# A decoder layer on one core: a softmax reciprocal moved behind the values' sums, the first pair's products in four banks, and one experts' product moved into slot 14

## The chip, the cores and the metric

The kernel runs on one core of a Trainium2 chip. The metric is the device time of one execution in microseconds. The kernel before was timed three times: 862.58, 862.88 and 864.7 us, median 862.88. A further execution was recorded by the hardware profiler. Its own time is 862.72 us, of which 860.9 us lie between its first and its last instruction (the span), so 1.8 us lie around the span.

The engines are PE (matrix products and transposes through the identity), DVE, ACT and POOL (elementwise work) and SP (which here only issues transfers). PEld is the part of PE that loads the stationary operand of a product.

## The reference

One decoder layer for 16 sequences of 128 tokens with 256 features, all in float32. Cut to what matters:

```python
x = x + self_attention(layernorm(x))        # 16 heads of 64, with biases, no mask
x = x + cross_attention(layernorm(x), ctx)  # 16 heads of 16, keys masked by position
x = x + experts(layernorm(x))

def experts(x):                             # 8 experts, 256 -> 512 -> 256
    logits = x @ gate_w.T + gate_b          # then RMS-normalized over the 8 experts
    g = max(softmax(logits / 0.5))          # the largest gate of each token
    norm_g = g / (g + 1e-6)
    h = gelu(einsum('nd,edh->neh', x, w1) + b1)
    y = einsum('neh,ehd->ned', h, w2) + b2  # every expert is computed for every token
    return (y * norm_g[:, None, None]).sum(axis=1)
```

## The kernel before

**Slots.** The first half of the span is attention. It is written as 16 slots, one for each sequence (a tile of 128 tokens). Slot s holds the self-attention of sequence s, the cross-attention queries and scores of sequence s-1, the cross-attention values of sequence s-2, and the projections for a coming pair of sequences. In the profile the first scores (L694) of slots 1, 2, 3, 13, 14 and 15 start at 49.06, 73.44, 100.81, 374.77, 401.91 and 427.19 us; a slot takes about 27.4 us. The second half of the span is the experts.

**The order is written out by hand.** Every step of a slot is an event with a name, and a table gives each name its due time: `DUE` for an ordinary slot, `FIRST_DUE` for slot 0, `SECOND_DUE` for three changes in slot 1. A slot has the length `SLOT`. `run_slots` takes all events in the order of their due times and lets each issue its instructions; on each engine the instructions then stand in exactly this order, and each engine works through its own in order. A smaller number in the table thus puts a step further ahead on its engine; the number itself is no time on the chip. A step that is due after the end of its slot lies between the steps of the next one: `xn=34.27` is 7.29 in the next slot.

**Pairs by seven products.** Queries, keys and values of two sequences are computed together with seven products of half-size blocks instead of eight (a Strassen scheme). For the values this is `paired_values`: four steps `v1x`, `v1y`, `v2x`, `v2y` on PE, one half of the heads per slot, and sums on ACT and DVE between them. For queries and keys it is `paired_steps`, with `q1x`, `q1y`, `q2x`, `q2y` and the same for k, and sums that carry the bias. The body for the values, cut:

```python
def first():                                   # v1x: bank with a and b
    product(1, v["a"]); product(6, v["b"])
    due("vu0", nc.scalar.copy, u[:, 0], v["a"])          # ACT
    plus("vu1", u[:, 0], u[:, 0], v["b"])                # DVE
def second():                                  # v1y: bank with f and e
    product(7, v["f"]); product(5, v["e"])
    plus("vu2", u[:, 1], u[:, 0], v["f"])
    plus("vu3", out[1][:, 1], u[:, 1], v["e"])
def third():                                   # v2x: product 2 onto a, then vc00 (ACT)
def fourth():                                  # v2y: product 4 onto f, product 3 onto e
```

Products 4 and 3 write onto the bank that `vu2` and `vu3` have read, so the first of them waits for `vu3`. In `paired_steps` the same place is `q2y` (or `k2y`), which waits for `qu3`, the sum written to `qT`. A float32 product is two PE rows in the trace, a transpose one.

**The softmax** (`softmax`, L395 to L416) has four steps for each half of eight heads: the negated maximum on DVE (`max0`), four exponentials with their sums on ACT (`ex0a`, `ex0b`), the reciprocal of the four sums on DVE (`r0a`, `r0b`, L412, `rinv`), and the normalization on POOL (`mul0a`, L416). The same names with c are cross-attention.

**Layer norms.** `bn` takes the statistics, `root` computes the inverse deviation with a chain of small DVE instructions (`inverse_root`, L323 to L338), and `xn` normalizes (L371). `LNx` transposes `xn` on PE (L380), and ACT copies the result (`LNxc`). `ab1` and `ab2` add a bias to `xs` on POOL, after the `xn` that reads it.

**PSUM.** Scores use four of the eight banks. All other products share four banks in the pool `ps_mm`; a tile gets a bank when the last reader of the tile in it is done. `ck` and `cke`, `cke2` are the cross-attention keys: the product and its four copies on ACT (L756, L767).

**Experts ahead of time.** The first 512 tokens' hidden values for 16 of 32 blocks are computed as plain products (`pre_hidden`, L1003, two products of 512 columns, four PE rows) while attention still runs. `PRE_STEPS` says which of them stand in which slot, by the event at whose due time they are issued and the event at which their bank is copied out: "qu1" means a copy on DVE, any other name one on ACT. The others stand in the tail, a stretch after slot 15 whose order is written out as calls.

Of the kernel before, what the change touches and what calls it, by code (L numbers as in the profile page):

```python
# [54 lines left out]
DUE = dict(  # L55
    S0=0.0, S1=1.0, T2a1=2.05, T2a2=2.49, T2a1e=2.69, ck=2.92, T2a2e=3.19, max0=3.47, v1x=3.79,
    cke=3.99, vu0=4.3, cke2=4.4, max1=4.61, v1y=4.66, q1x=5.52, ex0a=5.54, vu1=6.08, q1y=6.42,
    vu2=6.76, qu0=6.91, r0a=7.11, vu3=7.24, v2x=7.32, mul0a=7.39, vc00=7.4, ex0b=7.41, qu1=7.63,
    v2y=7.77, qu2=8.06, qu3=8.49, LNx=8.6, q2x=8.64, vc1=8.84, q2y=9.09, LNxc=9.1, ex1a=9.13,
    vc0=9.19, r0b=9.53, mul0b=9.81, qc1=10.19, cvr=10.21, qc00=10.51, qc0=10.54, r1a=10.98,  # L60
    T2b1=11.23, mul1a=11.26, cvre=11.31, ex1b=11.66, T2b2=11.66, T2b1e=11.86, CQ=12.1,
# [16 lines left out]
    r0a=-1.32, ex0b=-1.3, mul0a=-1.2, S1=-0.6, fv0e=0.1, r0b=0.15, mul0b=0.2, fab0=0.25,  # L78
# [3 lines left out]
    ve0=11.1, T1a2=11.34, T1a1e=11.54, T1b1=11.77, T1a2e=12.14, T1b2=12.21, LN1=12.64,  # L82
    T1b1e=12.74, LN1c=13.06, T1b2e=13.34, w0q=13.6, w0k=13.7, SVa=14.25, SVb=15.15, atT0=15.42,
    q1=17.2, atT1=17.21, wv0=17.3, q1e=17.6, k1=18.0, w1q=18.1, tf=18.2, SO=19.16, ke1=19.6,
    ws1=19.7, w1k=20.0, xsSO=22.81, bn=23.22, v1=23.47, ck=25.2, ve1=25.39, q1x=26.9, qu0=26.95,
    cke=27.0, cke2=27.01, q1y=27.8, qu1=28.2, k1x=28.7, qu2=28.8, qu3=29.2, root=29.25,
    xn=29.27, ab2=29.3, ku0=29.3, ab1=29.31, ku1=29.85, q2x=30.5, q2y=30.95, qc00=31.0,
    k1y=31.85, qc1=32.0, k2x=32.8, ku2=32.9, ku3=33.3, kc00=33.3, qc0=33.32, k2y=33.4, kc1=34.5,
    kc0=34.9,
)  # L90

SECOND_DUE = dict(wv1=4.7, st0=11.9, st1=12.46, st2=16.3, tf=19.6, st3=24.0)

PRE_STEPS = (
    (14, "q1x", "qc00"), (14, "k1x", "ku0"),
    (15, "v1x", "vu0"), (15, "q1x", "qu1"), (15, "k1x", "ku0"), (15, "k2x", "kc00"),
)
ON_ACT = ('T1a', 'T1b', 'T2a')
# [6 lines left out]
def decoder_layer(  # L105
# [53 lines left out]
    def psum_mm(name):  # L159
        return ps_mm.tile([P, 512], F32, tag="mm", name=name)  # L160
# [128 lines left out]
    def due(name, f, *a):  # L289

        if now[0] is None:
            with urgent():
                f(*a)
        else:
            at(name, f, *a)
# [449 lines left out]
    def cross_norm(b):  # L745
        xnT2 = work.tile([P, KD, 1, T], F32, tag="xnT2", name="xnT2")
        transpose_tokens([entry.pop(("xn", b))], xnT2, "LNxc")
        entry["xnT2", b] = xnT2
# [52 lines left out]
    def cross_queries(b):  # L801
        xnT2 = entry.pop(("xnT2", b))
        qT = work.tile([P, C2, T], F32, tag="q2T", name="q2T")
        mm = psum_mm("mm_q2")[:, : C2 * T].rearrange("p (m t) -> p m t", m=C2)
        for m in range(C2):
            for k in range(KD):
                nc.tensor.matmul(
                    mm[:, m, :],
                    wx[:, 0, k, m * P : (m + 1) * P],
                    xnT2[:, k, 0, :],  # L810
                    start=(k == 0),
                    stop=(k == KD - 1),
                )
        due(
            "q2T",
            nc.vector.tensor_tensor,
            qT, mm, bqk2[:, 0, :].unsqueeze(2).broadcast_to([P, C2, T]), ALU.add,
        )
        entry["q2T", b] = qT

    def cross_scores(b):


        qT, kT = entry.pop(("q2T", b)), entry.pop(("k2T", b))
        scs = [psum_sc(f"sc2_{n}") for n in range(2)]
        for m in range(C2):
            for r in range(4):
                rs = slice(32 * r, 32 * r + 32)
                nc.tensor.matmul(  # L829
                    scs[r // 2][:, r % 2, m * 2 * T : (m + 1) * 2 * T].rearrange(  # L830
                        "p (e t) -> p e t", e=2
                    ),
                    qT[rs, m, :],
                    kT[rs, m, :, :],
                    start=True,
                    stop=True,
                    tile_position=(32 * r, 0),
                )
        entry["sc2", b] = scs
# [13 lines left out]
    def cross_transposed(b, half, n):  # L853
        if n == 0:
            entry["cprT", b, half] = work.tile([P, 8, T], F32, tag="cprT", name="cprT")
        transposed(entry["cpr", b, half], entry["cprT", b, half], n, f"T2{'ab'[half]}{n + 1}e")

    def cross_values(b):


        v = v2s[b // GB % 2]
        prT = [entry.pop(("cprT", b, n)) for n in range(2)]
        po = psum_mm("po2")[:, : C2 * T].rearrange("p (m t) -> p m t", m=C2)
        for m in range(C2):
            for e in range(2):
                for r in range(4):
                    c0 = e * D + (4 * m + r) * 32
                    nc.tensor.matmul(  # L868
                        po[32 * r : 32 * r + 32, m, :],
                        v[:, b % GB, c0 : c0 + 32],  # L870
                        prT[r // 2][:, 4 * (r % 2) + 2 * m + e, :],
                        start=(e == 0),
                        stop=(e == 1),
                        tile_position=(0, 32 * r),
                    )
        atT = work.tile([P, C2, T], F32, tag="at2T", name="at2T")
        due(
            "at2T",
            nc.vector.tensor_tensor,
            atT, po, col(BV2, C2).unsqueeze(2).broadcast_to([P, C2, T]), ALU.add,  # L880
        )
        entry["at2T", b] = atT

    def cross_output(b):
        atT = entry.pop(("at2T", b))
        mm = psum_mm("mm_o2")
        for k in range(KD):
            nc.tensor.matmul(
                mm[:, :D], atT[:, k, :], wx_vo[:, 1, k, :], start=(k == 0), stop=(k == KD - 1)
            )  # L890
        due("xsCO", nc.vector.tensor_tensor, xs[:, b, :], mm[:, :D], xs[:, b, :], ALU.add)
# [29 lines left out]
    def expert_norm(b, copy=nc.scalar.copy):  # L921
        transpose_tokens(
            [entry.pop(("xn3", b))],
            xnT[:, :, b * T : (b + 1) * T].rearrange("p k (i t) -> p k i t", i=1),
            "LN3c",
            copy,
        )
# [67 lines left out]
    def pre_hidden(n, copy, name=None):  # L995

        p, i = n // 2, n % 2
        if n % 4 == 0:
            two = keep.tile([P, 2, 2, MT], F32, tag=f"k{(n // 4 + 3) % 4}", name="pre")
            pre[p], pre[p + 1] = two[:, 0], two[:, 1]  # L1000
        mm = psum_mm("mm_h")
        for k in range(KD):
            nc.tensor.matmul(  # L1003
                mm,
                w1q[p // (NP // QN)][:, i, k, p % (NP // QN)],
                xnT[:, k, :MT],
                start=(k == 0),
                stop=(k == KD - 1),
            )
        due(name, copy, pre[p][:, i], mm)  # L1010
# [150 lines left out]
    def sums():  # L1161
        return [ps_y.tile([P, 2, HT], F32, tag=f"y{n}", name=f"y{n}") for n in range(4)], set()
# [7 lines left out]
    def hidden_late(p):  # L1170
        for i in range(2):
            h = pre[p][:, i]
            nc.scalar.activation(h, h, AF.Gelu, bias=col(B1 + 2 * p + i))
# [13 lines left out]
    with tc.manual_schedule(  # L1187
        engines={mybir.EngineType.PE, mybir.EngineType.Activation}
    ):
        b = B - 1  # L1190
        a, v = nc.scalar.copy, nc.vector.tensor_copy
        for h in range(2):
            for n in range(2):
                cross_transposed(b - 1, h, n)
        pre_hidden(6, a)
        cross_values(b - 1)
        pre_hidden(7, a)
        cross_norm(b)
        cross_output(b - 1)
        expert_norm(b - 2)  # L1200
        cross_queries(b)
        pre_hidden(8, a)
        cross_scores(b)
        normalize_outputs(None, b - 1)
        pre_hidden(9, a)
        pre_hidden(10, a)
        cross_softmax(b)
        pre_hidden(11, v)
        expert_norm(b - 1, v)
        pre_hidden(12, v)  # L1210
        pre_hidden(13, v)
        for n in range(2):
            cross_transposed(b, 0, n)
        pre_hidden(14, v)
        pre_hidden(15, v)
        for n in range(2):
            cross_transposed(b, 1, n)
        scores.close()
        ps_y = ctx.enter_context(
            tc.tile_pool(name="ps_y", bufs=1, space=bass.MemoryType.PSUM, reuse_waits="tile")  # L1220
        )
        ys = sums()

        def late(p):
            hidden_late(p)
            for k in range(KD):
                summed_plain(k, p, ys)

        late(0)
        cross_values(b)  # L1230
        late(1)
        cross_output(b)
        normalize_outputs(None, b)
        late(2)
        late(3)
        expert_norm(b, v)
        late(4)
        for p in range(5, PRE):
            hidden_late(p)
# [285 lines left out]
```

## Time and profile before

| | |
|---|---|
| times | 862.58, 862.88, 864.7 us |
| profiled execution: its own time, its span | 862.72 us, 860.9 us |
| PE: matrix products | 847.6 us busy, 98% |
| PEld: weight loads | 719.4 us, 84% |
| DVE | 638.2 us, 74% |
| ACT | 474.1 us, 55% |
| POOL | 164.0 us, 19% |
| mean granted PE clock | 0.999 |
| stretch 100 to 380 us (slots 3 to 13) | busy in each 20 us: PE 19.9 to 20.0, DVE 15.6 to 18.1, ACT 12.6 to 16.6 |

A view of the profile gives, for an instruction or a group of equal ones: start, duration, engine, source line, operation, the tiles written and read, their sizes and the count; in brackets how long its engine had been idle before it and what released it. Matrix products overlap: the next one starts before the one before it has ended, and their ends are modelled. The time between the starts of two products, set against the usual time between such starts, therefore says more of what a wait costs than the idle time of PE does.

### The profile page before, as it was taken

What the parts mean: (1) busy time and instruction counts of PE and PEld (TensorE: products, weight loads), DVE (VectorE), ACT (ScalarE), POOL (GpSimd) and SP (SyncE); (2) the same over time, 40 slices, a digit from 0 to 9 for tenths busy, and PEclk for the clock granted to TensorE, in tenths of its full rate; (3) what the DMA queues carried; (4) which work ended last, traced back from release to release, by engine and by line L of the source; (5) the groups of instructions that cost most, each with busy time, mean ns of one, the idle gap of its engine ahead of it and who ended that gap; (6) DMA issues with size and microseconds to landing.
All of it is one profiled execution on the core that took longest, in us unless ns stands there. A gap on an engine that the chain in (4) does not pass through costs nothing.

```text
span 860.9 us, 16386 instructions
## 1 busy us (share of the span) xinstructions
PE 847.6 (98%) x5934; PEld 719.4 (84%) x5934; DVE 638.2 (74%) x1696; ACT 474.1 (55%) x1721; POOL 164.0 (19%) x179
## 2 busy tenths in 40 slices
PE   9999999999999999999999999999999999999997
PEld 7888888888888888888765558888888888888886
DVE  5788988889888879788667497776566756575655
ACT  4567677776867668676784613343334333444332
POOL 5133242423423243332431100000000000000000
PEclk9999999999999999999999999999999999999999
DMA  8400000000000000001141100000000000000000
GB/s 239 145 14 2 2 14 2 14 1 2 14 1 14 1 2 14 2 2 50 61 176 59 49 0 1 1 13 13 0 1 1 26 1 0 1 13 13 2 0 26
DMA packets 18321, 21.32 MB, mean 25 GB/s; under 512 B 9584, under 2 KB 13696, under 8 KB 17600
## 3 DMA queue, kind: packets, MB, share of 16 engines
q1 hardware_dynamic: 17728, 19.93, 7.3%
q8 instruction: 47, 0.77, 0.4%
q0 software_dynamic: 368, 0.30, 0.2%
q14 instruction: 34, 0.28, 0.1%
q10 hardware_dynamic: 144, 0.04, 0.0%
HBM read 18.16 MB, written 2.10 MB: 24 GB/s over the span
## 4 chain that ended last, share of the span: by engine, by line
PE 86%; DVE 7%; ACT 5%; issue 2%; DMA 0%; DVEq 0%; ACTq 0%
PE y L1266 19%; PE mm_qk L553 7%; PE mm_o L739 6%; PE tr_p L431 6%; PE he L1266 5%; PE hf L1266 5%; PE ha L1266 5%; PE sc L694 4%; PE mm_v L644 3%; PE po L719 3%; PE mm_h L1003 3%; ACT pr L401 3%; PE hb L1266 3%; PE po L868 2%; PE sc L829 2%; PE mm_qk L488 2%
## 5 line engine op out<-in xcount | busy, mean ns | idle before, releaser
L401 ACT ACTIVATE cpr<-sc,nmax 128x128 f32<-128x128 f32 x256 | 90.5, 403 | 17.3 <-DVE nmax L395 13.9
L401 ACT ACTIVATE pr<-sc,nmax 128x128 f32<-128x128 f32 x256 | 92.6, 404 | 2.6 <-DVE nmax L395 2.6
L416 POOL TENSOR_TENSOR cpr<-cpr,rinv 128x512 f32<-128x512 f32 x64 | 65.5, 1039 | 127.4 <-DVE rinv L412 127.3
L1295 ACT ACTIVATE h<-u,colv 128x256 f32<-128x256 f32 x56 | 28.4, 508 | 93.8 <-DVE u L1282 92.0
L395 DVE TENSOR_REDUCE nmax<-sc 128x8 f32<-128x1024 f32 x64 | 76.4, 1214 | 0.2 <-PE sc L694 0.2
L416 POOL TENSOR_TENSOR pr<-pr,rinv 128x512 f32<-128x512 f32 x64 | 67.1, 1049 | 43.4 <-DVE rinv L412 40.4
L1296 DVE TENSOR_TENSOR c<-u,hf 128x256 f32<-128x256 f32 x56 | 23.5, 420 | 69.3 <-PE hf L1266 69.3
L1266 PE MATMUL hf<-xt,w 128*128 128x256 f32 x224 | 66.8, 380 | 0.4 <-DVE u L1281 0.4
L1279 ACT COPY u<-ha 128x256 f32<-128x256 f32 x56 | 20.8, 372 | 84.0 <-PE ha L1266 84.0
L1266 PE MATMUL ha<-xnT,w 128*128 128x256 f32 x224 | 66.6, 379 | 0.0
L1266 PE MATMUL y<-t,w 128*128 128x256 f32 x224 | 66.6, 380 | 0.0
L401 ACT ACTIVATION_READ_ACCUMULATOR pr<-sc,nmax 128x1 f32 x256 | 62.4, 244 | 0.0
L401 ACT ACTIVATION_READ_ACCUMULATOR cpr<-sc,nmax 128x1 f32 x256 | 62.2, 243 | 0.0
L739 PE MATMUL mm_o<-wo,atT 128*128 128x256 f32 x256 | 58.1, 380 | 0.2 <-DVE atT L313 0.2
L1266 PE MATMUL y<-h,w 128*128 128x256 f32 x224 | 57.6, 379 | 0.0
L739 PEld LDWEIGHTS mm_o<-wo,atT 128*128 128x128 f32 x256 | 47.6, 190 | 7.3 <-issue 1.0
L384 POOL TENSOR_TENSOR xs<-xs,rowv 128x256 f32<-128x256 f32 x32 | 23.3, 740 | 139.0 <-ACT v L313 72.1
L1266 PEld LDWEIGHTS ha<-xnT,w 128*128 128x128 f32 x224 | 42.6, 190 | 7.1 <-issue 1.2
L1266 PEld LDWEIGHTS hf<-xt,w 128*128 128x128 f32 x224 | 42.4, 190 | 6.7 <-DVE u L1281 1.0
L1266 PEld LDWEIGHTS y<-h,w 128*128 128x128 f32 x224 | 42.6, 190 | 5.8
L1266 PEld LDWEIGHTS y<-t,w 128*128 128x128 f32 x224 | 41.9, 190 | 6.2 <-issue 0.8
L313 DVE COPY_PREDICATED_SCALAR sc<-hidden_keys,masked 128x1024 f32 x30 | 38.4, 1279 | 9.3 <-PE sc L829 9.0
(251 smaller groups left out, 2072.6 us busy)
## 6 DMA issues: line engine op xcount, KB each, us to landing
w<-in_w SPq DMA_DIRECT2D x8, 1024.0 KB, 5.1
ctx<-in_ctxT SPq DMA_DIRECT2D x8, 256.0 KB, 2.6
out_x<-ot SPq DMA_DIRECT2D x8, 256.0 KB, 2.1
xs<-in_x SPq DMA_DIRECT2D x3, 512.0 KB, 6.2
wk<-in_wk SPq DMA_DIRECT2D x2, 512.0 KB, 6.9
wq<-in_wq SPq DMA_DIRECT2D x2, 512.0 KB, 7.8
wv<-in_wv SPq DMA_DIRECT2D x2, 512.0 KB, 9.7
wo<-in_wo SPq DMA_DIRECT2D x1, 1024.0 KB, 8.1
```

What stands on the lines that cost most here:

```text
L313: f(*a)
L395: nc.vector.tensor_reduce(w["nmax"], sc, AX.X, ALU.max, negate=True)
L401: nc.scalar.activation(w["pr"][:, i, :], sc[:, i, :], AF.Exp, bias=w["nmax"][:, i : i + 1], scale=1.0, accum_out=sums[:, j : j + 1],)
L416: nc.gpsimd.tensor_tensor(four, four, w["rinv", n].unsqueeze(2).broadcast_to([P, 4, T]), ALU.mult)
L431: nc.tensor.transpose(tr[:, j, :], w["pr"][:, 4 * n + j, :], ident)
L553: nc.tensor.matmul(out[:, q, :], paired[x, n][m - 1][:, q], paired[b0][m - 1], start=clears and q == 0, stop=True, skip_group_check=True,)
L644: nc.tensor.matmul(out, paired[b0][m - 1], paired["v", n][m - 1], start=clears, stop=True, skip_group_check=True,)
L694: nc.tensor.matmul(sc[:, j, c * T : (c + 1) * T], qT[r, c, :], kT[r, c, :], start=True, stop=True,)
L719: nc.tensor.matmul(po[j * DH1 : (j + 1) * DH1, c, :], v[:, h * DH1 : (h + 1) * DH1], prT[:, 4 * j + c, :], start=True, stop=True,)
L739: nc.tensor.matmul(mm[:, :D], atT[:, c, :], wo[:, c, :], start=(c == 0), stop=(c == C1 - 1))
L1266: nc.tensor.matmul(out, left[p // q][n - 1][:, p % q], rights[n - 1], **flags)
L1295: nc.scalar.activation(h[:, 1, 1], u[:, 3], AF.Gelu, bias=col(B1 + 2 * p + 1))
```

## The change

Four edits, all of them to the order:

- In `DUE`, `r0a` (the reciprocal of the first four sums of a slot) moves from 7.11 to 7.32. It then stands on DVE behind `vu3` (7.24) and, in all slots that have it, also behind the `xn` of the sequence before (7.29).
- In `FIRST_DUE`, `k1y` moves from 31.85 to 28.9, in front of `q2x`, so that the four first steps of queries and keys of the first pair stand together and hold four banks; `ku2`, `ku3` and `qc0` move forward with it, and the copies of the keys (`cke`, `cke2`) move in front of `qu0` on ACT.
- In `FIRST_DUE`, `root` and `xn` of slot 0 move from 29.25 and 29.27 to 24.79 and 25.0, in front of the first pair's sums on DVE; `ab2` and `ab1` move with them on POOL.
- In `PRE_STEPS`, slot 14 gets a third product at the due time of `q2x`, copied by ACT at `qc00`; the one at `q1x` is now copied by DVE at `qu1`. All later ones move up by one, and the call `pre_hidden(6, a)` between the transposes and the values of sequence 14 in the tail is gone.

```diff
 DUE = dict(
...
-    vu2=6.76, qu0=6.91, r0a=7.11, vu3=7.24, v2x=7.32, mul0a=7.39, vc00=7.4, ex0b=7.41, qu1=7.63,
+    vu2=6.76, qu0=6.91, vu3=7.24, r0a=7.32, v2x=7.32, mul0a=7.39, vc00=7.4, ex0b=7.41, qu1=7.63,
...
 FIRST_DUE = dict(
...
-    ws1=19.7, w1k=20.0, xsSO=22.81, bn=23.22, v1=23.47, ck=25.2, ve1=25.39, q1x=26.9, qu0=26.95,
-    cke=27.0, cke2=27.01, q1y=27.8, qu1=28.2, k1x=28.7, qu2=28.8, qu3=29.2, root=29.25,
-    xn=29.27, ab2=29.3, ku0=29.3, ab1=29.31, ku1=29.85, q2x=30.5, q2y=30.95, qc00=31.0,
-    k1y=31.85, qc1=32.0, k2x=32.8, ku2=32.9, ku3=33.3, kc00=33.3, qc0=33.32, k2y=33.4, kc1=34.5,
-    kc0=34.9,
+    ws1=19.7, w1k=20.0, xsSO=22.81, bn=23.22, v1=23.47, root=24.79, xn=25.0, ck=25.2, ve1=25.39,
+    q1x=26.9, cke=26.9, cke2=26.91, qu0=26.95, q1y=27.8, qu1=28.2, ab2=28.44, ab1=28.5,
+    k1x=28.7, qu2=28.8, k1y=28.9, qu3=29.2, ku0=29.3, ku1=29.85, ku2=30.0, ku3=30.1, q2x=30.5,
+    q2y=30.95, qc00=31.0, qc1=32.0, qc0=32.5, k2x=32.8, kc00=33.3, k2y=33.4, kc1=34.5, kc0=34.9,
 )
...
 PRE_STEPS = (
-    (14, "q1x", "qc00"), (14, "k1x", "ku0"),
+    (14, "q1x", "qu1"), (14, "q2x", "qc00"), (14, "k1x", "ku0"),
     (15, "v1x", "vu0"), (15, "q1x", "qu1"), (15, "k1x", "ku0"), (15, "k2x", "kc00"),
 )
...
                 cross_transposed(b - 1, h, n)
-        pre_hidden(6, a)
         cross_values(b - 1)
         pre_hidden(7, a)
```

The line numbers in all views of the kernel before are those of its own file. The changed file is one line shorter from the tables on, and two lines shorter in the tail.

## The prediction

> **What bounds the kernel now.** I read the page first. PE is busy all the time, at full clock, so a change of order can only win what PE loses in waits, and loses where it makes PE wait.
>
> ```profile
> PE 847.6 (98%) x5934; PEld 719.4 (84%) x5934; DVE 638.2 (74%) x1696; ACT 474.1 (55%) x1721; POOL 164.0 (19%) x179
> PEclk9999999999999999999999999999999999999999
> ```
>
> Next, the list of PE's waits (line waited with, releaser: total, times, longest). Three of its longest lie at places that the change touches.
>
> ```profile
> PE tr_x L380 <- DVE xn L371: 1.7, 1, 1.7
> ...
> PE mm_q L807 <- ACT pre L313: 0.7, 1, 0.7
> PE mm_qk L553 <- DVE su L313: 0.5, 1, 0.5
> ```
>
> The list shows little of the wait that comes in every slot. The view of the values' line L644 shows it: some products last 484 ns instead of 379, and the weight loads in front of them waited 6.0 us for `v` (the sum `vu3`).
>
> ```profile
> L644 PE MATMUL mm_v<-wv,sums_v x32: 379/379/484, 52.9 to 410.3; 128*128 128x256 f32 x32
> ...
>   DVE v L313: 6.0, 12
> ```
>
> The timeline of slot 13 (start, length) shows how it comes about.
>
> ```profile
> 382.02 0.66 ACT L564 ACTIVATE su<-mm_qk,colv 128x128 f32<-128x128 f32 x2
> 382.09 0.60 PE L644 MATMUL mm_v<-wv,xnT 128*128 128x256 f32 x2
> 382.27 0.18 DVE L412 RECIPROCAL rinv<-sums 128x4 f32<-128x4 f32 x1 [0.80 <-ACT pr L401]
> 382.36 0.39 DVE L313 TENSOR_TENSOR v<-sv,mm_v 128x256 f32<-128x256 f32 x1
> 382.67 0.41 DVE L371 TENSOR_SCALAR xn<-xs,mv,root 128x256 f32<-128x256 f32 x1
> ...
> 382.81 0.30 PEld L644 LDWEIGHTS mm_v<-wv,sums_v 128*128 128x128 f32 x2 [0.53 <-DVE v L313]
> 382.81 0.70 PE L644 MATMUL mm_v<-wv,sums_v 128*128 128x256 f32 x2
> ...
> 382.99 0.94 DVE L313 TENSOR_TENSOR su<-su,mm_qk 128x256 f32<-128x256 f32 x2
> ...
> 383.34 0.59 PE L644 MATMUL mm_v<-sums_v,xnT 128*128 128x256 f32 x2
> ...
> 383.77 0.38 PE L380 MATMUL tr_x<-ident,xn 128*128 128x128 f32 x2
> ...
> 383.97 0.42 DVE L313 TENSOR_TENSOR qT<-su,mm_qk 128x256 f32<-128x256 f32 x1
> ```
>
> DVE stood idle 0.80 us in front of the reciprocal, whose sums ACT had not finished; `vu3`, ready long before, was queued behind it, and PE waited for `vu3`.
>
> **The sum, part by part.** It is made against the profiled execution's 862.72 us (span 860.9 and 1.8 around it), 0.16 below the median of 862.88, so the answer stands for either.
>
> *The reciprocal behind `vu3`, slots 1 to 14.* An unhindered values' product takes 0.43 us of PE (383.34 to 383.77). After the one at 382.09 the next could have started at 382.52; it started at 382.81, 0.29 late, and took 0.53 itself (to 383.34), 0.10 more, since its weights were not loaded ahead. That is 0.39 a slot. With the reciprocal gone from the front, `vu3` and `xn` fill DVE's idle 0.80 us (0.39 + 0.41), `vu3` is done near 381.9, and the wait is gone. The reciprocal itself loses nothing: it starts when ACT's sums come, 382.27, when `xn` has ended. Queued behind it on POOL are `ab2` and `mul0a`; `ab2` waits for `xn` anyway, so both come earlier.
>
> The Trainium skill, "TensorE: Matmul & The Clock Gate", section "Step-by-step: what each phase is for", says that PE pulls weight loads ahead of running products. By it alone the 0.10 would be no loss, and the 14 slots would hold 1.4 us less. The row disagrees: a load that waits for a semaphore started with its product, at 382.81.
>
> What is late next: the queries' `q2y`, which waits for `qu3` (the `qT` row). `qu1` stood behind `xn` until 382.99. Now it waits for ACT's `qu0` alone, which ends at 382.68; with 0.10 between ACT's end and DVE's start, 382.78, so `qT` ends 0.21 earlier, near 384.18 instead of 384.39. PE comes 0.39 earlier. In the trace `q2y`'s product starts at 384.44, 0.05 after `qT`, its weight load with it, so 0.10 is lost there already. After: load at 384.23, 0.10 for it, 384.33, where PE could go on at 384.44 - 0.39 = 384.05, a loss of 0.28. So 0.18 of the 0.39 is handed back, and 0.21 stays. Slots 1 to 13: 13 x 0.21 = 2.7 us. In four of these PE has no slack at a later step either (`at2T` ends 0.10 to 0.11 before its use at 118.33, 173.07 and 200.76; `atT` is waited for at 94.95): I take those as giving back all, 4 x 0.2 = 0.8. That leaves 1.9, with bounds 0 (all handed back) and 13 x 0.39 = 5.1 (none).
>
> *Slot 14* has no `q2y`. Its wait at `vu3` is longer (idle 0.197 instead of 0.123): 0.46 won.
>
> *The first pair.* The two L553 waits stand here:
>
> ```profile
> 45.74 0.61 PE L553 MATMUL mm_qk<-sums_v,sums_k 128*128 128x128 f32 x4
> ...
> 46.86 0.71 PE L553 MATMUL mm_qk<-xnT,wk 128*128 128x128 f32 x4 [0.51 <-DVE su L313]
> ...
> 47.98 0.71 PE L553 MATMUL mm_qk<-sums_v,wk 128*128 128x128 f32 x4 [0.40 <-DVE kT L313]
> ```
>
> Products here follow at 0.45 (45.29, 45.74). The one at 46.86 is 0.67 late and 0.10 longer, the one at 47.98 0.57 and 0.10: 1.44 us. The cause is on DVE: the 13 instructions of `root` and `xn` (44.16 to 46.48, 2.3 us) stand between the queries' and the keys' sums. They move to 40.04, when the statistics end; DVE is idle from there for 2.81 us, so they cost nothing; without that cover it would be their 2.3. On ACT the four key copies (1.50 us) come first: the product `mm_k` ends at 41.26, so `qu0` starts near 42.8 instead of 42.19, 0.6 later. Then `qu1` ends near 43.9 and `qu3` near 44.9. PE reaches `q2x` after eight first-step products, 41.09 + 8 x 0.45 = 44.7, and `q2y` at 45.1: covered, by 0.2 at the least. `k1y` needs the fourth bank, which `mm_k` frees near 42.8, and comes at 43.8. The keys' sums follow at the same pace. 1.44 won, bounds 0.7 (one of the two waits stays) and 1.5.
>
> *Slot 14's added product* is work moved, not added: four PE rows, 1.81 us (455.34 to 457.15 in the tail). Where it goes, PE waited 0.68 at 413.78 for ACT's copy of the product at `q1x`; by the starts 0.95. That copy now is 0.68 us on DVE, inside the 0.90 us that DVE was idle there, and releases the bank. The new product's copy takes the old place on ACT (to 413.72), and PE reaches `mm_q` 1.81 later than it could, so the wait is gone: 0.95, bounds 0 and 1.0.
>
> *Slot 15.* `xn` now stands in front of the reciprocal that waited for ACT until 435.71, so the 1.73 wait at `tr_x` (1.9 by the starts) goes. But the copy of `pre` on DVE stays behind that reciprocal (to 436.79) and holds a bank for the transposes, and ACT's copy of `tr_x` stays behind its exponentials (to 437.26) and holds `mm_q`. The wait moves a few steps on; I take 0.1, bounds -0.3 and 1.9.
>
> *The tail.* The removed call covered this:
>
> ```profile
> 453.59 1.91 PE L431 MATMUL tr_p<-ident,cpr 128*128 128x128 f32 x16
> ...
> 455.34 1.88 PE L1003 MATMUL mm_h<-xnT,w 128*128 128x512 f32 x4
> 455.42 1.28 DVE L293 COPY cprT<-tr_p 128x512 f32<-128x512 f32 x2
> ...
> 457.15 0.54 PE L868 MATMUL po<-cprT,v 128*32 128x128 f32 x12
> ```
>
> `po` needs both DVE copies. They end at 456.70; with 0.05 and 0.10 PE goes on at 456.85 instead of 455.34, less 0.15 for the first rows that need only ACT's copies: 1.35 lost, bounds 1.0 and 1.8.
>
> SP's and POOL's orders stay, and no transfer moves. Sum: 1.9 + 0.46 + 1.44 + 0.95 + 0.1 - 1.35 = 3.5, rounded up to 3.6 since the 0.21 is nearer to 0.22: 859.1 us.
>
> **Rivals.** (1) *All handed back in the slots*: ACT and DVE, not PE, pace a slot, and 1.9 becomes 0. For it: 0.18 of 0.39 goes at the first step already; against: DVE's idle 0.80 is really filled. 3.5 - 1.9 = 1.6 won, 861.1. (2) *Nothing handed back*: `qu3` is early enough, 5.1 instead of 1.9: 6.8 won, 855.9. Against it is the chain from ACT above. (3) *Slower: DVE blocked by POOL.* In slot 4 the two `xn` from 114.75 take 1.43 together, the second 1.13 instead of 0.40, because POOL's product runs from 114.91. `xn3` at 386.50 starts 0.25 after POOL's `mul0b` ends (386.25). It follows PE, which gains 0.21, while `mul0b` follows ACT: a margin of 0.04. If POOL is later than that, `xn3` is held by up to 0.73, `q2T` behind it (end 388.71, use 389.05) reaches PE about 0.5 late, in 13 slots 6.5: 862.7 - 3.6 + 6.5 = 865.6. It decides once `mul0b` ends after `xn3` could begin; against it, ACT and with it POOL also start earlier. The Trainium skill ("SBUF — State Buffer", section "SBUF: two separate sides") describes that block as an exclusive lock held for the whole instruction; the 1.13 row agrees. (4) *The edit doesn't act*: another wait holds `vu3`. `vu3`'s operands were ready 0.80 us earlier, so this is within (1).
>
> **Numbers.** Forecast 0.74, (1) with (4) 0.14, (2) 0.07, (3) 0.05. A measurement of this kernel can tell about 0.3% from no change, 2.6 us: faster means under 860.3. The forecast's own range, from the bounds of slots and tail, is 857.4 to 860.5. Stretched to case (1) it is 857.4 to 861.3 and leaves out (2) and (3). Faster 0.74 x 0.97 + 0.07 = 0.79; same 0.14 + 0.02 = 0.16; slower 0.05.
>
> **What would show it.** Right: no 484 ns among L644's products after slot 0; slots of about 27.2 instead of 27.4; L553 waits of the first pair gone and a longer loss at `q2y`; no wait at `mm_q` in slot 14; a wait of over 1 us for `cprT` at L868 in the tail. Wrong: slots as long as before, a second long `xn` in every slot, or waits in slots 14 and 15 that add up to more than before.

## The result, and the profile after

The changed kernel takes 858.35 us (median of 6 runs, 858.1 to 858.56) against 862.79 us for the kernel before in the same batch (6 runs): 4.44 us less. The ratio, estimated from all runs and not from the medians, is 0.9945, 95% interval 0.9932 to 0.9957. The prediction was 859.1, with a range of 857.4 to 861.3. The profiled execution took 858.56 us, its span is 856.8. The code that the traces name stands one line higher than before (L644 is now L643, L553 is L552, L807 is L806), in the experts' part two lines.

**The values' line.** In the view of L643 the long products are gone: all last 379 ns, none 484. PE no longer waits there for `v`. DVE now waits in front of `su` (the sum `qu1`), 3.6 us in 13 slots, and the view puts that down to a product of this line.

```profile
L643 PE MATMUL mm_v<-wv,sums_v x32: 379/379/379, 51.7 to 405.8; 128*128 128x256 f32 x32
...
  DVE su L312: 3.6, 13
```

The wait is for ACT all the same. ACT's `su` (`qu0`), onto which `qu1` adds, ends here within 0.02 us of that product, and DVE starts 0.03 after it. In experiment 1 the profile names ACT, and in experiment 9 DVE's `su` starts before the product has ended (378.56 and 378.64), again 0.03 after ACT's. The row of experiment 1:

```profile
380.66 0.42 DVE L313 TENSOR_TENSOR su<-su,mm_qk 128x256 f32<-128x256 f32 x1 [0.27 <-ACT su L564]
```

**Slot 13.** The timeline (start, length) shows `vu3` and `xn` where DVE had stood idle, the reciprocal directly behind them, and what is late next.

```profile
377.79 0.42 DVE L312 TENSOR_TENSOR v<-sv,mm_v 128x256 f32<-128x256 f32 x1
...
378.13 0.41 DVE L370 TENSOR_SCALAR xn<-xs,mv,root 128x256 f32<-128x256 f32 x1
...
378.32 0.66 ACT L563 ACTIVATE su<-mm_qk,colv 128x128 f32<-128x128 f32 x2
...
378.56 0.18 DVE L411 RECIPROCAL rinv<-sums 128x4 f32<-128x4 f32 x1
...
378.81 0.59 PE L643 MATMUL mm_v<-wv,sums_v 128*128 128x256 f32 x2
379.01 0.94 DVE L312 TENSOR_TENSOR su<-su,mm_qk 128x256 f32<-128x256 f32 x2 [0.27 <-PE mm_v L643]
...
379.99 0.42 DVE L312 TENSOR_TENSOR qT<-su,mm_qk 128x256 f32<-128x256 f32 x1
...
380.46 0.52 PEld L552 LDWEIGHTS mm_qk<-sums_v,wq 128*128 128x128 f32 x4
380.46 0.71 PE L552 MATMUL mm_qk<-sums_v,wq 128*128 128x128 f32 x4
```

The values' products now follow at 0.43 (378.38 to 378.81). At `q2y` the weight load still starts with its product, 0.05 after `qT` has ended (379.99 + 0.42 = 380.41). The product before it began at 379.89, and products there follow at 0.45, so PE could have gone on at 380.34: 0.12 is lost to the wait, and as before 0.10 to the weights.

**The other places.** The list of PE's waits no longer has `tr_x` with 1.7, `mm_q` with 0.7 or the two waits of the first pair. In their place stand the waits that slot 15's gain turned into (`v`, `pre`) and the tail's `cprT`. The longest new one, for `wk`, is a transfer at the start, before anything that the change touches.

```profile
PE mm_qk L487 <- DMA wk<-in_wk: 0.8, 1, 0.8
PE tr_p L430 <- ACT v L312: 0.6, 1, 0.6
PE po L867 <- DVE cprT L292: 0.5, 2, 0.3
PE tr_p L430 <- DVE pre L312: 0.5, 1, 0.5
...
PE mm_o L738 <- DVE atT L312: 0.3, 1, 0.3
```

In the timeline of the first pair the keys' products that began at 46.86 and 47.98 begin at 46.43 and 46.88, 0.45 apart and 0.61 long:

```profile
46.43 0.61 PE L552 MATMUL mm_qk<-xnT,wk 128*128 128x128 f32 x4
...
46.88 0.61 PE L552 MATMUL mm_qk<-sums_v,wk 128*128 128x128 f32 x4
```

In the tail's timeline `po` now stands behind DVE's copies:

```profile
451.69 1.28 DVE L292 COPY cprT<-tr_p 128x512 f32<-128x512 f32 x2
...
452.43 0.41 PE L867 MATMUL po<-cprT,v 128*32 128x128 f32 x2 [0.30 <-DVE cprT L292]
...
453.03 0.64 PE L867 MATMUL po<-cprT,v 128*32 128x128 f32 x15 [0.19 <-DVE cprT L292]
```

**The account.** The table compares the starts of the same PE instructions in the two profiled executions. Plus is later. The added and removed product is set at four rows of 0.43 (1.72) in both places.

| stage | predicted us | measured us |
|---|---|---|
| up to the first pair (start, transfer of `wk`) | 0 | +0.43 |
| first pair | -1.44 | -1.62 |
| slot 1 | in the next line | 0.0 |
| slots 2 to 13 | -1.9 | -2.78 |
| slot 14: `vu3`, `mm_q` | -0.46, -0.95 | -0.46, -0.95 |
| slot 15 | -0.1 | 0.0 |
| tail, `po` | +1.35 | +1.30 |

The marks that this is read from: the scores that began at 49.06, 73.44, 401.91 and 427.19 us begin 1.20, 1.19, 3.97 and 3.71 us earlier, PE's last instruction 4.12. Another 0.05 us is won in small steps of slot 14 that the table leaves out. The start of the program scatters: over the profiles of this study the first slot's scores lie between 12.67 and 14.66 us. A scatter of this size is enough for the two profiles to differ by 4.1 and the medians by 4.44; how the unprofiled executions started is not recorded.

### The profile page after: what moved, and what is told of

Read it like the earlier page. It is cut to its first block, busy times and chain, and to the rows that moved or that the text cites. A ratio compares the mean times of both kernels' runs of the same rounds, so it can differ in the third digit from the quotient of the medians.

```text
span 856.8 us, 16387 instructions
## 1 busy us (share of the span) xinstructions
PE 846.4 (99%) x5934; PEld 721.0 (84%) x5934; DVE 642.6 (75%) x1697; ACT 473.7 (55%) x1720; POOL 164.1 (19%) x179
## 4 chain that ended last, share of the span: by engine, by line
PE 90%; DVE 6%; ACT 2%; issue 1%; DMA 1%; DVEq 0%; SPq 0%
PE y L1264 19%; PE mm_qk L552 10%; PE mm_o L738 6%; PE tr_p L430 6%; PE he L1264 5%; PE hf L1264 5%; PE ha L1264 5%; PE mm_v L643 5%; PE sc L693 4%; PE po L718 3%; PE mm_h L1002 3%; PE hb L1264 3%; PE po L867 2%; PE sc L828 2%; PE mm_qk L487 2%; PE mm_k L755 2%
```

## The experiments

Times are medians; "before" is the kernel before in the same batch (863.0 to 863.1 us). The changed kernel was measured in its own batch, so distances from it (858.35) are between batches. For experiments 5, 6 and 9 the interval of the ratio overlaps that of the changed kernel, so what they gain on it rests on the steps in their traces as much as on the medians. Where a trace is set against another, the steps are read from a mark behind the program's start.

**1. The reciprocal alone.**

```diff
-    vu2=6.76, qu0=6.91, r0a=7.11, vu3=7.24, v2x=7.32,
+    vu2=6.76, qu0=6.91, vu3=7.24, r0a=7.32, v2x=7.32,
```

> The kernel before with only the reciprocal moved behind the values' sums. My theory (a slot's wait for vu3 goes, part of it comes back at q2y and at at2T or atT): as in the changed kernel's trace, slots 1 to 13 give 2.8 us; slot 14 gives 0.46 at vu3, but without the added product the wait at mm_q for ACT's copy takes it back; slot 15's wait at tr_x turns into others. In all 2.8 us faster than before, ratio 0.9968, and no values' product of L644 at 484 ns after slot 0. Rival 1 (all handed back): ratio 1.000. Rival 2 (nothing handed back): 5 us, ratio 0.994.

Measured: 860.16 us, ratio 0.9965 (0.9953 to 0.9977), 2.9 us faster than before. From 73.44 to 401.91 the scores gain 2.67 us. In slot 14 PE gains 0.46 at `vu3` and loses 0.47 at `mm_q`, where ACT's copy still ends the wait; in slot 15 it gains 1.90 at `tr_x` and loses 1.88 at the places after it. So part of the gain comes back at `q2y`, but not all, and slot 14's 0.46 counts only together with the added product.

**2. The first pair alone.** Only the new times of `FIRST_DUE`.

```diff
+    ws1=19.7, w1k=20.0, xsSO=22.81, bn=23.22, v1=23.47, root=24.79, xn=25.0, ck=25.2, ve1=25.39,
+    q1x=26.9, cke=26.9, cke2=26.91, qu0=26.95, q1y=27.8, qu1=28.2, ab2=28.44, ab1=28.5,
...
```

> The kernel before with only the first pair's new times (root and xn at the front, four banks, the keys' copies first). Theory: the two L553 waits go and the pair ends 1.6 us earlier, as in the changed kernel's trace (1.4 by the prediction), and nothing later takes it back: ratio 0.9981. Rival: the following slots, still with their waits at vu3, are paced by ACT and DVE and not by PE's start, so part is given back: ratio 0.999 to 1.000.

Measured: 861.5 us, ratio 0.998 (0.9971 to 0.9989), 1.6 us faster. Its profiled execution was its slowest (863.16 us) and reached the first slot's scores 1.93 us later than the one before; from the pair's first product to slot 1's scores PE gains 1.63 us, and over the 13 slots that follow only 0.14 of it fades. The slots do not take it back.

**3. `root` and `xn` alone.**

```diff
-    ws1=19.7, w1k=20.0, xsSO=22.81, bn=23.22, v1=23.47, ck=25.2,
+    ws1=19.7, w1k=20.0, xsSO=22.81, bn=23.22, v1=23.47, root=24.79, xn=25.0, ck=25.2,
...
-    root=29.25, xn=29.27,
```

> The kernel before with only root and xn at the front of the first pair's sums; the steps' order on PE and the copies' order on ACT stay as before. Theory as the prediction put it (the 13 instructions of root and xn on DVE are the cause): the whole 1.4 to 1.6 us of the first pair, ratio 0.9982. Rival: without the fourth bank and with the keys' sums still behind the queries' q2y, PE still waits at one of the two L553 places, about 0.6 us won, ratio 0.9993.

Measured: 862.57 us, ratio 0.9995 (0.9986 to 1.0004): 0.5 us faster, but the interval holds no change as well. PE's timeline shows one of the two places cured and the other not:

```profile
46.42 0.61 PE L553 MATMUL mm_qk<-xnT,wk 128*128 128x128 f32 x4
47.55 0.71 PE L553 MATMUL mm_qk<-sums_v,wk 128*128 128x128 f32 x4 [0.52 <-DVE kT L313]
```

The first wait goes (0.78 with its weights), the second grows by 0.12. With DVE free, the keys' second sum (`ku2`, at 46.62) waits 0.47 us for PE's `k1y`, which stands behind the queries' `q2y`, and the third (`kT`) follows it. In experiment 2, where `k1y` stands in a fourth bank ahead of the queries' second steps, that wait is gone; the copies that moved on ACT with it were not tried apart. The instructions of `root` on DVE explain 0.66 of the pair's 1.62 us (0.78 less 0.12), not all.

**4. The experts' product alone.**

```diff
-    (14, "q1x", "qc00"), (14, "k1x", "ku0"),
+    (14, "q1x", "qu1"), (14, "q2x", "qc00"), (14, "k1x", "ku0"),
...
-        pre_hidden(6, a)
```

> The kernel before with only the experts' product moved from the tail into slot 14. Theory (the prediction's terms): 0.95 us won at mm_q in slot 14, 1.3 to 1.35 lost in the tail where the product covered the copies of cprT: 0.35 to 0.4 us slower, ratio 1.0004. Rival: the tail's loss is covered otherwise (DVE's copies come earlier as well), and 0.95 us stay: ratio 0.9989.

Measured: 863.5 us, ratio 1.0007 (0.9998 to 1.0016); the interval holds no change as well. The trace gives the two terms apart: 0.95 won at `mm_q`, 1.30 lost at `po`. By itself this part of the change costs 0.35 us. The three parts alone sum to -2.9 - 1.6 + 0.4 = -4.1; together they give 4.4, 0.3 more. By the traces the difference is slot 14's 0.46, which is handed on at `mm_q` unless the added product has freed that place.

**5. The tail's products shifted.** One product stands in front of `po` again, and a later place gives one up.

```diff
+        pre_hidden(7, a)
         cross_values(b - 1)
-        pre_hidden(7, a)
+        pre_hidden(8, a)
...
         cross_queries(b)
-        pre_hidden(8, a)
+        pre_hidden(9, a)
...
-        pre_hidden(9, a)
         pre_hidden(10, a)
```

> The changed kernel with the tail's products shifted: one stands between the last transposes and po again, each later place gets the next product, and the place behind normalize_outputs has one instead of two. Theory (po waits 1.3 us for DVE's two copies of cprT because no product covers them): the two waits at L867 go, 1.3 us won there; later one product less lies between the scores and the transposes of the last cross-attention, which may cost 0.4 us there; 0.9 us faster than the changed kernel, 857.5, ratio to before 0.9938. Rival (the cover is only moved, the last transposes then wait as long for POOL): 858.4, ratio 0.9948.

Measured: 857.51 us, ratio 0.9937 (0.9923 to 0.995), 0.8 us under the changed kernel. Against the changed kernel's trace 1.30 us goes at `po`, and 0.58 comes back at the last transposes, which now wait for POOL (0.52 by the start, 0.06 by a longer first transpose). The tail's loss is a cover taken away, and most of it can be had back.

**6. Slot 15's first copy on DVE.**

```diff
-    (15, "v1x", "vu0"), (15, "q1x", "qu1"),
+    (15, "v1x", "vu1"), (15, "q1x", "qu1"),
...
-                copy = nc.vector.tensor_copy if out == "qu1" else nc.scalar.copy
+                copy = nc.vector.tensor_copy if out in ("qu1", "vu1") else nc.scalar.copy
```

> The changed kernel; in slot 15 the copy of the first product goes to DVE (behind vu1's place) instead of ACT. Theory (slot 15 is paced by ACT: its copy of 0.58 us stands in front of the first exponentials, so that the reciprocal, DVE's copy of pre, ACT's copies of xnT and v are all late by that much, and the 1.9 us won at tr_x come back as 0.65, 0.34 and 0.87): these waits shrink by about 0.5 each, 1.2 to 1.5 us won, 857.0, ratio 0.9931. Rival (the product's copy then delays DVE instead, or the bank comes free no earlier): no change, 858.4, ratio 0.9948.

Measured: 857.01 us, ratio 0.9932 (0.992 to 0.9944), 1.3 us under the changed kernel. In the changed kernel's timeline of slot 15 ACT's copy stands in front of the exponentials, and DVE's reciprocal and its copy of `pre` come late:

```profile
429.21 0.58 ACT L312 COPY pre<-mm_h 128x512 f32<-128x512 f32 x1 [0.91 <-PE mm_h L1002]
...
432.09 0.66 DVE L312 COPY pre<-mm_h 128x512 f32<-128x512 f32 x1
...
432.90 0.63 PE L430 MATMUL tr_p<-ident,cpr 128*128 128x128 f32 x4 [0.49 <-DVE pre L312]
```

With the copy on DVE the same places read:

```profile
428.87 0.38 ACT L400 ACTIVATE pr<-sc,nmax 128x128 f32<-128x128 f32 x1
...
430.92 0.69 DVE L312 COPY pre<-mm_h 128x512 f32<-128x512 f32 x1 [0.26 <-PE mm_h L1002]
```

The exponentials start at 428.87 instead of 430.38, since ACT is rid of the copy and of the 0.91 us that it stood idle in front of it for the product. At the three places PE gains 0.65, 0.35 and 0.49 us: 1.5. ACT's order held slot 15 in the changed kernel: DVE's reciprocal waited for ACT's sums. Of the wait for ACT's `v`, 0.12 us is left.

**7. Both of these** ("both covers" below).

> The changed kernel with both edits, the tail's products shifted and slot 15's first copy on DVE. The two lie in different stages, so the gains should add: 0.9 + 1.4 = 2.3 us, 856.1, ratio 0.9921. Rival (slot 15's earlier end only meets the tail's waits for DVE and POOL, which follow their own pace): as the better of the two alone, 857.0, ratio 0.9931.

Measured: 856.0 us, ratio 0.9921 (0.9907 to 0.9934): the gains add. It is the fastest version of the study, 7.0 us under the kernel before and 2.35 under the changed kernel (between batches; the intervals of the two ratios just touch).

**8. `xn3` in front of `qc0`.**

```diff
-    xn3=37.78,
+    xn3=37.3,
```

> The changed kernel with xn3 on DVE in front of qc0 instead of behind it, so that it could start about 0.28 us before POOL's product mul0b ends. Theory (rival 3 of the prediction: DVE's xn is held while POOL's product runs): xn3 lasts 0.68 instead of 0.40 us in slots 2 to 13, everything behind it on DVE comes 0.28 later, q2T has 0.2 to 0.3 of slack, so the time changes by 0 to 1.5 us, ratio 0.9948 to 0.9966. Rival (no such block in this place): xn3 lasts 0.40, ratio 0.9948.

Measured: 862.15 us, ratio 0.9988 (0.9979 to 0.9997), 3.8 us over the changed kernel. Neither theory holds. The timeline of POOL, DVE and PE in one slot:

```profile
384.36 1.04 POOL L415 TENSOR_TENSOR pr<-pr,rinv 128x512 f32<-128x512 f32 x1 [0.89 <-DVE rinv L411]
...
385.12 0.43 DVE L370 TENSOR_SCALAR xn<-xs,mv,root 128x256 f32<-128x256 f32 x1
...
386.25 0.63 PE L430 MATMUL tr_p<-ident,cpr 128*128 128x128 f32 x4 [0.20 <-ACT qT L563]
```

`xn` runs for 0.28 us beside POOL's product (to 385.40) and lasts 0.43, not 0.68. The time went elsewhere: `qc0`, now behind `xn`, ends at 386.07, 0.35 us later than it would have, and the transposes that need its bank start 0.36 late. On average 0.34 of that stays in slots 3 to 13 (11 x 0.34 = 3.8). The profile names ACT's `qT` as releaser (to 386.10), but in the changed kernel the same transpose begins at 382.76, before ACT's `qT` has ended (382.97). What fits in both is `qc0`, which ends 0.16 and 0.18 before the transpose, and whose end is the one that the edit moved. What it costs to put an operation in front of another on DVE was in this place the queue, not a block by POOL.

**9 and 10. The cross keys earlier.** These shorten what ACT does in front of `qu0`.

```diff
-    ck=2.92, cke=3.99, cke2=4.4,
+    ck=1.9, cke=2.6, cke2=3.3,      # keys before transposes
+    ck=0.95, cke=2.6, cke2=2.65,    # keys before scores
```

> The changed kernel with the cross keys (mm_k) on PE in front of the two transposes of cprT instead of behind them, and their two ACT copies k2T earlier (the first in front of cprT's copies, the second in front of the values' copy). ACT then has less to do in front of the first exponentials. Theory (what q2y hands back in each slot, 0.12 us of waiting and 0.10 of an unloaded weight, hangs on ACT: k2T, exponentials and qu0 follow each other without a gap and qu1 to qu3 come behind): the exponentials and qu0 start 0.1 us earlier, q2y waits 0.1 less; 13 times 0.1 = 1.3 us faster than the changed kernel, 857.1, ratio 0.9933, and up to 2.8 us where the weights are loaded ahead again. Rival (the wait hangs on something else, PE's own products or the bank): 858.4, ratio 0.9948 or slower.

> The changed kernel with the cross keys on PE still earlier, between the two halves of the self scores, and both k2T copies in front of cprT's. Theory: qu0 and with it qT end some 0.5 us earlier, more than q2y waits: all of 0.22 goes in 13 slots, 2.8 us; the second scores, 0.9 us later, are early enough for their maximum, and what else comes later is unknown, up to 0.1 us a slot: 857.0 to 855.6, ratio 0.9931 to 0.9916. Rival (DVE's maximum of the second scores comes later and with it the second exponentials and S1's transposes): 858.4 or slower, ratio 0.9948 or more.

Measured: keys before transposes 857.75 us, ratio 0.9937 (0.9924 to 0.9951); keys before scores 863.18 us, ratio 1.0001 (0.9993 to 1.001). The theory on `q2y` holds: in slot 13 of the two traces PE gains 0.11 and 0.22 us there against the changed kernel. That it would shorten the slots does not. The first edit loses 0.05 where the products now stand and the rest at later steps, and from slot 1 to slot 14 nothing is won; its 0.6 us lie in slot 15, where ACT's chain is what PE waits for. The second loses 0.39 a slot where the keys' products (128 rows, 128x128) stand between scores of 64 rows, and at the cross queries that follow `q2y` another 0.16 (slot 13); with the 0.22 won in between, a slot is 0.32 to 0.42 us longer. The timeline with the keys inside the scores:

```profile
376.00 0.97 PEld L755 LDWEIGHTS mm_k<-ctx,wx 128*128 128x128 f32 x8
376.00 1.16 PE L755 MATMUL mm_k<-ctx,wx 128*128 128x128 f32 x8
377.09 0.52 PEld L693 LDWEIGHTS sc<-kT,qT 64*128 64x128 f32 x8
377.09 0.60 PE L693 MATMUL sc<-kT,qT 64*128 64x128 f32 x6
```

Each load starts with its product, and around each of the two changes of shape the products follow at 0.20 to 0.21 instead of 0.11, twice: four times 0.10. Where the same products follow transposes of their own shape, in the changed kernel, the load runs 0.11 ahead (373.86 and 373.97).

**11. All three.** Both covers, and the keys before the transposes.

> The kernel with both covers and, in addition, the cross keys in front of the transposes of cprT. The earlier keys gave 0.6 us on the changed kernel, nearly all of it in slot 15, where ACT's chain came earlier. Theory (slot 15's waits hang on ACT's chain as a whole, so two edits that shorten the same chain share the gain): the slots' own 0.05 and part of slot 15 remain, 0.2 to 0.5 us faster than both covers, 855.7, ratio 0.9916. Rival (the edits' gains add): 855.4, ratio 0.9914; or the chain is no longer what slot 15 waits for: 856.0, ratio 0.9921.

Measured: 856.57 us, ratio 0.9925 (0.9912 to 0.9939): not faster than both covers without it. The traces say why nothing is left of the 0.6 us. In the changed kernel ACT stood idle 0.91 us in front of its copy of the experts' product; the earlier keys filled that gap to 0.11, and so brought the exponentials forward. With the copy on DVE there is no such gap to fill. Slot 15 still waits for ACT: the wait for its copy `v` is 0.12 us with both covers and 0.24 here, where the exponentials start 0.13 later after the slot's first scores.

## Why the prediction was right, point by point

**The wait at `vu3`** was 0.39 a slot, and 0.39 was won at that place: 0.29 of waiting and 0.10 of the weights, in each of slots 2 to 13. The weights' 0.10 was a real loss: the product gets 0.10 shorter as soon as its wait goes, and at `q2y`, where a wait stays, the 0.10 stays.

**The hand-back at `q2y`** was the right mechanism, and its size was off: 0.12 instead of 0.18. The mis-sized term is the 0.10 between ACT's end and DVE's start, which measured 0.03 (ACT's `su` ends at 378.98, DVE's starts at 379.01). The profile before already held it. The 0.10 is what the reciprocal's row shows, behind ACT's read of the sums (382.17 to 382.27), whereas `su` behind ACT's `su` started after 0.03 wherever it waited for it, as the keys' sum in slot 3 (124.06 to 124.09). `qT` so ended 0.27 earlier, not 0.21, and 0.27 stayed in each slot. Experiments 9 and 10 show that this wait hangs on ACT's work in front of `qu0`.

**The four tight steps** gave back less than the whole. At the wait for `atT` 0.12 came back and in the slots of the other three 0.11 each, 0.45 in all instead of 0.8; in the last of them half of it came at a later place, the use of `atT` at 204.70. Slot 1 was counted as a full slot and gave nothing: its wait at `vu3` was short (0.045 idle), the 0.31 won there came back as 0.21 at `q2y` and 0.1 at the cross scores (61.88). So 12 x 0.27 - 0.45 = 2.8 where the sum had 1.9. This term is the largest error of the sum, and within its bounds. Three errors make up the difference: the 0.10 left out 0.7 of the gain and the price of the tight steps 0.35, while slot 1 added 0.2 that never came. That they cancel in part is luck.

**The first pair** gave 1.62 instead of 1.44, since a loss of 0.18 at the queries' `q2y` (44.30 before), which the sum had not counted, went too. The reason given was half of it: experiment 3 shows that DVE's 13 instructions account for one of the two waits; the other goes only with the rest of the edit, `k1y` in the fourth bank. The lower bound of 0.7 "one of the two waits stays" is what that experiment met.

**Slot 14 and the tail** came as worked out: 0.46, 0.95 and 1.30 for 1.35. The sign of a wait of over 1 us for `cprT` holds by the starts alone; PE's idle time there adds up to 0.5. **Slot 15** moved on as forecast; the third wait, for ACT's copy `v` of the cross values' rows (0.87 with its weights), was not named. Experiment 6 shows that 1.5 of their 1.9 us came from an order on ACT, which a reader of the profile before could have seen in the copy that stands in front of slot 15's exponentials.

**The rivals.** (1) and (2) are both refuted by the slots, which kept 0.27 of 0.39. (3) did not happen: in the changed kernel `xn3` starts 0.24 us after POOL's product has ended (382.28 and 382.52 in slot 13), not 0.04. Experiment 8 shows that its price was wrong as well: an overlap of 0.28 us with the end of POOL's product costs 0.02. (The rows from 114.75 that it was read from lie in slot 3, not 4.) An earlier `xn3` would have cost through the queue behind it.

## What to carry to other kernels

Where an engine that runs in order waits for one producer while work that is ready stands behind it, the gain of a swap is the consumer's wait plus the unloaded weights, less what the next wait on the same consumer takes back; work out that next wait from its own chain, and take the handoff (from one engine's end to the start of what waits for it on another) from a row of the same pair of operations, since here 0.07 us too much of it, in each of 12 slots, made most of the largest error. A gain at a place whose releaser is another busy engine (slot 15) moves on to the next wait until that engine's own queue is shortened. Work that is taken away from a place where PE is full is not free if it covered somebody else's copies.

## What the runs showed of the hardware that was not expected

**POOL and `xn`.** The six long `xn` (1.13 us) and the one of experiment 8 (0.43) fit one rule: where POOL's product began first, DVE's `xn` ends 0.15 us after it. In the changed kernel POOL's product from 113.40 lasts to 114.52 and the second `xn` from 113.54 to 114.67; in experiment 8 POOL ends at 385.40 and `xn` at 385.55. With 0.41 us for an unhindered `xn`, an overlap of under 0.26 us should cost nothing, by estimate (0.41 less 0.15); a shorter overlap with such a product, 0.15 us at 411.89 in the kernel before, costs nothing (`xn` lasts 0.39). Where `xn` began first, as at 113.24, 0.16 before POOL's product, it lasted 0.38. The Trainium skill, "SBUF — State Buffer", section "SBUF: two separate sides", calls it an exclusive lock held for the whole instruction; the rows agree with that, and add that its price for `xn` is POOL's remaining time less about 0.26.

**A change between products of 64 and of 128 rows** cost 0.20 us, 0.10 at each of the two products around it, with the weight load starting together with its product. The Trainium skill, "TensorEngine Tiling (Array Packing)", section "Key Properties", says that changing the tiling mode drains the engine; the 0.39 us of two such changes in each of slots 2 to 13 of experiment 10 agree with that, though the rows show the time and not the draining itself. A product that is used to fill a gap between such scores pays for both changes.

**ACT to DVE.** In the kernel before, DVE started 0.03 us after the end of an ACT activation that it waited for (all 13 `su`, and 40 times in the experts' part), but mostly (42 of 47 cases) 0.10 us after ACT's read of the sums that a reciprocal waited for.
